# Selective scan on one core: Softplus summed in PSUM, a fifth of GpSimd's output multiplies on VectorE, a fourth scan buffer

## The chip, the cores and the metric

The kernel runs on one core of one Trainium2 chip. The metric is device time in microseconds (us) of one execution. A core has four engines that compute, each with a queue of its own that it works off in order: TensorE (PE in the profile; PEld is its weight load), VectorE (DVE), ScalarE (ACT) and GpSimd (POOL). A fifth, SyncE (SP), issues the DMAs here. [...]

## The reference

Sixteen images of 64 x 64 positions and 96 channels pass through two blocks.

The first block normalises, widens the image, squares it between two linear layers and narrows it again; the second block normalises, projects 96 channels to twice 192, convolves 3 x 3, applies SiLU, and then scans the image in four directions (rows, columns, and both reversed). In each direction there are 192 channels with 16 states each:

```
delta = softplus(dts + dt_bias)
h = exp(delta * A) * h + (delta * u) * B
y = sum over the 16 states of h * C
```

B, C and dts are linear in the image and differ from position to position. The four directions are added, normalised, gated with SiLU(z) and projected back to 96 channels.

## The kernel before, in words

`front(mi)` makes the first block, the convolution and z of image mi; `finish(mi)` makes the normalisation, gate and projection of its scan; `scan()` runs over all sixteen images and takes the largest part of the time. While it scans image mi, `front(mi + 1)` and then `finish(mi - 1)` run in the background.

**The scan's units.** An image is scanned in 8 steps (pair 0 forwards over four stretches of T = 1024 positions, pair 1 backwards). A step has 6 blocks (`blocks`, L601), a block has NQ = 4 groups (L705). So there are 16 x 8 x 6 x 4 = 3072 groups, numbered n. A group holds 128 partitions (32 channels times 4 states) by two halves e = 1 and e = 0 by 1024 positions. For each group:

- `drive(n)`, L731: GpSimd multiplies dtu by B into the buffer b, both halves at once (128x2048). The pool of b has three buffers (L613).
- `decay(n, e)`, L725: ScalarE makes da = exp(delta * a) for a half, into one of two PSUM tiles.
- `recur(n, e, out)`, L740 forwards and L742 backwards: VectorE's scan instruction over a half. For e = 1 the states go over b in SBUF, for e = 0 over da in PSUM.
- `keep(n, e, h)`, L748: ScalarE copies the last state of the half for the next stretch, one element per partition. The last of the four stretches needs none.
- The multiply by C: GpSimd for e = 1, in place in b (L877); VectorE for e = 0, from da into b (L887).
- `read_out(n)`, L764: TensorE adds the states up with a 0/1 matrix, 16 matmuls (y in PSUM over the four groups of a block; for pair 1 an identity matmul, L757, first puts in the partial sum y0 of pair 0). `store(n)`, L775, copies y out once per block.

**The order.** Instructions are put in each engine's queue as the Python code runs. The loop at L833 does, for group n: scan e=1, its keep, decay (n+1, 1), read-out of n-1, the multiply on GpSimd, drive n+2; then scan e=0, the multiply on VectorE, its keep, decay (n+1, 0). A drive has to wait for the read-out that frees its buffer.

**Positions.** At three places in each group `slot(0)`, `slot(1)` and `slot(2)` advance the background work by one `yield` each: first the step's own generator, `project` (L622), which makes rows (B and C), delta and dtu of the next step, then `front` or `finish`. `project` works in two halves of TB = 512 positions. In each half: load three tiles u (L634), three positions, matmul pp (L640), one position, pr (L643), and then for three tiles v: matmul s (L650), Softplus, dtu and delta to DRAM (L676, L677). So there are 128 x 2 x 3 = 768 such tiles.

**Softplus** is computed as max(s, 0) + log(1 + e) plus a correction e - ((1 + e) - 1) for the rounding of 1 + e, with e = exp(-|s|): ScalarE makes Abs, Exp, Ln and 1 + e (L658 to L661, L666); VectorE does the rest (L664, L668, L669) and multiplies by u (L672).

**Loads.** Everything goes through SyncE's queue in the order of the code. `fetch` brings dtu and delta of the next block, spread over the 128 partitions; `fetch_bc` brings a row block of B or C; `fetch_y0` brings the partial sum. In `front`, the narrowed rows s come from DRAM in two SBUF tiles of 44 and 20 rows (L408 to L416).

Of the kernel before, what the change touches and what calls it, by code (L numbers as in the profile page):

```python
# [74 lines left out]
PSLICES = 60  # L75


@with_exitstack
def tile_two_blocks(
# [103 lines left out]
    b12 = ctx.enter_context(tc.tile_pool(name="b12", bufs=1))  # L183
# [56 lines left out]
    def front(mi):  # L240
# [72 lines left out]
        for p0 in range(0, UPS, PP):  # L313
# [94 lines left out]
        JS = 44  # L408
        s = [
            b18.tile([UPS, JS, C], F32, name="s0", tag="b18"), b12.tile([UPS, HW - JS, C], F32, name="s1", tag="b12")  # L410
        ]
        for _ in range(2):
            yield
        for i, n, first in [(0, JS // 4, k * JS // 4) for k in range(4)] + [(1, 10, 0), (1, 10, 10)]:
            nc.sync.dma_start(out=s[i][:, first:first + n, :], in_=s_d[:, JS * i + first:JS * i + first + n, :])
            yield  # L416
# [4 lines left out]
        for j0 in range(0, HW + 8, 8):  # L421
            if done is not None:
                nc.scalar.activation(
                    x1v[:, :, j0 - 8:j0], done.rearrange("c w h -> c h w"), AF.Identity, bias=shift
                )
            if j0 < HW:
# [5 lines left out]
                for j in range(8):  # L432
                    nc.tensor.matmul(
                        done[:, j, :], lhsT=s[(j0 + j) // JS][:, (j0 + j) % JS, :], rhs=down_s, start=False, stop=True,
                        skip_group_check=True,
                    )
# [169 lines left out]
    def scan():  # L606


        with ExitStack() as es:
# [3 lines left out]
            p3 = es.enter_context(tc.tile_pool(name="sc_3", bufs=3))  # L613
# [8 lines left out]
            def project(mi, pair, lc, out):  # L622
# [6 lines left out]
                xs_d = image[mi]["xs"]  # L629
                for t in range(0, T, TB):  # L630
                    u = []
                    for v in range(3):
                        uv = up_.tile([128, TB], F32, name="u")
                        nc.sync.dma_start(out=uv, in_=xs_d[v, :, lc * T + t:lc * T + t + TB])  # L634
                        u.append(uv)
                    for _ in range(3):
                        yield
                    pp = gps.tile([128, TB], F32, name="pp", tag="g")
                    for v in range(3):
                        nc.tensor.matmul(pp, lhsT=xpt_s[:, pair, v, :], rhs=u[v], start=(v == 0), stop=(v == 2))  # L640
                    yield
# [4 lines left out]
                    for i, v in enumerate((0, 2, 1)):  # L646
# [10 lines left out]
                        e, d = (pj.tile([128, TB], F32, name=k) for k in ("e", "d"))  # L657
                        nc.scalar.activation(e, s, AF.Abs)  # L658
                        nc.scalar.activation(e, e, AF.Exp, scale=-1.0)
                        yield  # L660
                        nc.scalar.activation(d, e, AF.Ln, bias=one_s)  # L661
                        for _ in range(2):
                            yield
                        nc.vector.scalar_tensor_tensor(d, s, 0.0, d, ALU.max, ALU.add)  # L664
                        yield
                        nc.scalar.activation(s, e, AF.Identity, bias=one_s)  # L666
                        yield
                        nc.vector.scalar_tensor_tensor(s, s, -1.0, e, ALU.add, ALU.subtract)  # L668
                        nc.vector.tensor_sub(s, d, s)  # L669
# [3 lines left out]
                        yield  # L673
# [3 lines left out]
                        nc.sync.dma_start(out=out["delta"][v][:, t:t + TB], in_=delta)  # L677

            def fetch(what, ctx, bi):

                v, s0, r = blocks[bi]
                t = p2.tile([128, 2, T], F32, name=what)
                for e in (1, 0):
                    nc.sync.dma_start(
                        out=t[:, e, :],
                        in_=ctx[what][v][32 * (s0 + e):32 * (s0 + e) + 32, :].unsqueeze(1).to_broadcast([32, NQ, T]),
                    )
# [40 lines left out]
            def drive(n):  # L728
                b = p3.tile([128, 2, T], F32, name="b")
# [14 lines left out]
            def keep(n, e, h):  # L744
                st, bi, j = units[n]
                if st % NT < NT - 1:
                    end = h[:, T - 1:T] if steps[st][1] == 0 else h[:, 0:1]
                    nc.scalar.copy(states[bi][1][:, e, j:j + 1], end)  # L748
# [84 lines left out]
            for n, (st, bi, j) in enumerate(units):  # L833
# [28 lines left out]
                elif j == 1:  # L862
                    if ahead:
                        ops["delta", m + 1] = fetch("delta", *ahead)
                    if n + NQ <= last and steps[units[n + NQ - 1][0]][1] == 1:
                        st2, bi2, _ = units[n + NQ - 1]
# [151 lines left out]
```

## Time and profile before

| | us |
|---|---|
| median of three runs | 21924.01 (21922.5 to 21927.97) |
| the profiled execution, its own time | 21910.69 |
| its span, first to last instruction | 21908.9 |
| GpSimd busy | 20900.4 |
| VectorE busy | 19849.9 |
| TensorE busy | 15342.2 |
| ScalarE busy | 13130.2 |

A row of the groups reads: line, engine, operation, output <- inputs, their shapes, how often | busy time in us, mean duration in ns | idle time of the engine just before, and what ended it. A row of the waits reads: who waited for whom: us in total, how often, the longest. A row of the timeline reads: start in us, duration in us, what, and in brackets the idle time before it. A row of the busy times in a stretch reads: the stretch, its length, then busy us and number of instructions of PE, PEld, DVE, ACT and POOL, the granted TensorE clock, the DMA share and GB/s. TensorE's fp32 matmuls leave two records each. The end of a matmul's record is modelled, so a busy TensorE is not one at its peak.

### The profile page before, as it was taken

What the parts mean: (1) busy time and instruction counts of PE and PEld (TensorE: products, weight loads), DVE (VectorE), ACT (ScalarE), POOL (GpSimd) and SP (SyncE); (2) the same over time, 40 slices, a digit from 0 to 9 for tenths busy, and PEclk for the clock granted to TensorE, in tenths of its full rate; (3) what the DMA queues carried; (4) which work ended last, traced back from release to release, by engine and by line L of the source; (5) the groups of instructions that cost most, each with busy time, mean ns of one, the idle gap of its engine ahead of it and who ended that gap; (6) DMA issues with size and microseconds to landing.
All of it is one profiled execution on the core that took longest, in us unless ns stands there. A gap on an engine that the chain in (4) does not pass through costs nothing.

```text
span 21908.9 us, 260666 instructions
## 1 busy us (share of the span) xinstructions
PE 15342.2 (70%) x92844; PEld 6324.7 (29%) x92844; DVE 19849.9 (91%) x12829; ACT 13130.2 (60%) x20854; POOL 20900.4 (95%) x6152
## 2 busy tenths in 40 slices
PE   6766767766777677777767677767777677677745
PEld 4322323232232322324233232322323223242211
DVE  0999999999999999999999999999999999999996
ACT  4665656666565665656656566665656656566543
POOL 0999999999999999999999999999999999999997
PEclk7776777877778777777877778777787877778856
DMA  2555565656656566565655656556565655656654
GB/s 80 190 191 188 193 214 194 209 195 200 205 191 215 189 206 201 192 215 192 207 198 194 214 192 209 196 201 206 193 211 189 210 199 198 206 195 208 210 177 134
DMA packets 1851895, 4276.30 MB, mean 195 GB/s; under 512 B 449118, under 2 KB 548350, under 8 KB 1848542
## 3 DMA queue, kind: packets, MB, share of 16 engines
q1 hardware_dynamic: 1850590, 4259.62, 58.1%
q8 instruction: 731, 11.98, 0.2%
q14 instruction: 574, 4.70, 0.1%
HBM read 3380.58 MB, written 878.18 MB: 194 GB/s over the span
## 4 chain that ended last, share of the span: by engine, by line
DVE 36%; POOL 19%; issue 18%; PE 9%; ACT 9%; DMA 7%; SPq 1%; POOLq 0%; DVEq 0%; ACTq 0%
POOL b L731 10%; POOL b L877 10%; DVE da L742 7%; DVE da L740 7%; DVE b L740 6%; DVE b L742 6%; DVE b L887 4%; ACT da L725 4%; DMA u<-xs_d 2%; DVE s L669 2%; DVE dtu L672 2%; DVE s L668 2%; PE y L764 1%; DMA ct<-rows 1%; PE pp L640 1%
## 5 line engine op out<-in xcount | busy, mean ns | idle before, releaser
L731 POOL TENSOR_TENSOR b<-dtu,bt 128x2048 f32<-128x2048 f32 x3072 | 13984.9, 4552 | 584.6 <-DMA dtu<-dtu_d 522.9
L725 ACT ACTIVATE da<-delta,a_s 128x1024 f32<-128x1024 f32 x6144 | 6853.5, 1116 | 2826.6 <-DVE b L887 1185.9
L877 POOL TENSOR_TENSOR b<-b,ct 128x1024 f32<-128x1024 f32 x3072 | 7309.1, 2379 | 259.8 <-ACT new L748 249.5
L764 PE MATMUL y<-b,fold_s 128*32 128x256 f32 x49152 | 4638.9, 492 | 4107.3 <-DVE b L887 3102.6
L887 DVE TENSOR_TENSOR b<-da,ct 128x1024 f32<-128x1024 f32 x3072 | 3752.6, 1222 | 84.5
L764 PEld LDWEIGHTS y<-b,fold_s 128*32 128x32 f32 x49152 | 1353.3, 126 | 7627.7 <-DVE b L887 4083.3
L740 DVE TENSOR_TENSOR_SCAN da<-da,new,b 128x1024 f32<-128x1024 f32 x1152 | 2694.3, 2339 | 252.3 <-ACT da L725 252.3
L740 DVE TENSOR_TENSOR_SCAN b<-da,new,b 128x1024 f32<-128x1024 f32 x1152 | 2698.0, 2342 | 174.1 <-POOL b L731 166.9
L742 DVE TENSOR_TENSOR_SCAN da<-da,new,b 128x1024 f32<-128x1024 f32 x1152 | 2693.8, 2338 | 172.9 <-ACT da L725 172.7
L742 DVE TENSOR_TENSOR_SCAN b<-da,new,b 128x1024 f32<-128x1024 f32 x1152 | 2697.1, 2341 | 151.6 <-POOL b L731 109.5
L748 ACT COPY new<-da 128x1 f32<-128x1 f32 x2304 | 362.3, 157 | 3028.5 <-DVE b L887 3023.2
L473 PE MATMUL c_ps<-xgp,wtap_s 96*128 96x512 f32 (+1 forms) x4608 | 1817.8, 675 | 168.9 <-ACT row L491 164.1
L650 PE MATMUL s<-pr,dtw_s 128*128 128x512 f32 x1536 | 1120.4, 819 | 557.8 <-ACT delta L674 516.7
L377 PE MATMUL o_ps<-w2c_s,hsq 128*100 128x96 f32 x9600 | 1205.3, 293 | 191.9 <-ACT hsq L348 180.1
L365 PE MATMUL h_ps<-xu,w1t_s 96*128 96x500 f32 x1920 | 1147.6, 700 | 244.2 <-ACT hsq L348 108.6
L748 ACT COPY new<-b 128x1 f32<-128x1 f32 x2304 | 432.6, 188 | 1445.7 <-DVE b L742 740.4
L377 PEld LDWEIGHTS o_ps<-w2c_s,hsq 128*100 128x100 f32 x9600 | 1119.5, 203 | 407.4 <-ACT hsq L348 227.7
L640 PE MATMUL pp<-u,xpt_s 128*128 128x512 f32 x1536 | 903.7, 734 | 224.2 <-DMA u<-xs_d 216.0
L742 DVE TENSOR_TENSOR_SCAN b<-da,b 128x1024 f32<-128x1024 f32 x384 | 876.7, 2283 | 133.2 <-ACT da L725 74.8
L473 PEld LDWEIGHTS c_ps<-xgp,wtap_s 96*128 96x128 f32 (+1 forms) x4608 | 631.9, 182 | 1193.3 <-issue 938.6
L740 DVE TENSOR_TENSOR_SCAN da<-da,b 128x1024 f32<-128x1024 f32 x384 | 875.8, 2281 | 106.9 <-ACT da L725 106.9
L742 DVE TENSOR_TENSOR_SCAN da<-da,b 128x1024 f32<-128x1024 f32 x384 | 876.0, 2281 | 105.0 <-ACT da L725 105.0
(120 smaller groups left out, 18077.1 us busy)
## 6 DMA issues: line engine op xcount, KB each, us to landing
dtu<-dtu_d SPq DMA_DIRECT2D x1536, 512.0 KB
delta<-delta_d SPq DMA_DIRECT2D x1536, 512.0 KB
bt<-rows SPq DMA_DIRECT2D x1024, 512.0 KB
ct<-rows SPq DMA_DIRECT2D x1024, 512.0 KB
u<-xs_d SPq DMA_DIRECT2D x896, 256.0 KB
dtu_d<-dtu SPq DMA_DIRECT2D x768, 256.0 KB
delta_d<-delta SPq DMA_DIRECT2D x768, 256.0 KB
xr<-in_x SPq DMA_DIRECT2D x768, 128.0 KB
```

What stands on the lines that cost most here:

```text
L365: nc.tensor.matmul(h_ps[j], lhsT=w1t_s[:, 128 * j:128 * (j + 1)], rhs=xu.rearrange("c p q -> c (p q)"), start=True, stop=True,)
L377: nc.tensor.matmul(o_ps[:, p, :], lhsT=hsq[j][:, UPS * p:UPS * (p + 1)], rhs=w2c_s[:, j, :], start=(j == 0), stop=(j == HB - 1),)
L473: nc.tensor.matmul(c_ps[p:p + n], lhsT=wtap_s[:, tap, 128 * i:128 * i + n], rhs=xgp[:, h0:h0 + 8, dx:dx + HW], start=(tap == 0), stop=(tap ...
L640: nc.tensor.matmul(pp, lhsT=xpt_s[:, pair, v, :], rhs=u[v], start=(v == 0), stop=(v == 2))
L650: nc.tensor.matmul(s, lhsT=dtw_s[:, pair, v, :], rhs=pr, start=True, stop=True)
L725: nc.scalar.activation(da, ops["delta", n // NQ][:, e, :], AF.Exp, scale=a_s[:, k, g, units[n][2]:units[n][2] + 1])
L731: nc.gpsimd.tensor_mul(b, ops["dtu", n // NQ], bt.unsqueeze(1).to_broadcast([128, 2, T]))
L740: nc.vector.tensor_tensor_scan(out, da, b, before, ALU.mult, ALU.add)
L742: nc.vector.tensor_tensor_scan(out[:, ::-1], da[:, ::-1], b[:, ::-1], before, ALU.mult, ALU.add)
L764: nc.tensor.matmul(y[32 * q:32 * q + 32, e, :], lhsT=fold_s, rhs=b[:, e, QT * q:QT * q + QT], start=(pair == 0 and j == 0 and e == 0), sto ...
L877: nc.gpsimd.tensor_mul(h, h, bc[1, r, j])
L887: nc.vector.tensor_mul(bs[n][:, 0, :], h, bc[1, r, j])
```

## The change

1. **Softplus.** VectorE's three instructions go. ScalarE makes m = max(s, 0) (Relu), w = 1 + e and then w = 1 - w; TensorE adds w + e + d + m in PSUM with four identity matmuls. VectorE multiplies the sum by u as before, and ScalarE copies it to delta in the same position.
2. **A shared multiply.** With `SHARE = 5`, in each group with n % 5 == 4 the e=1 scan writes into da (PSUM), and VectorE multiplies by C into b, in place of GpSimd.
3. **End states.** In the other groups VectorE copies the e=1 end state, in place of ScalarE.
4. **Read-out.** `read_out(n - 2)` takes the place of `read_out(n - 1)`, `store` follows it, and b has four buffers. y0 is asked for at the end of a block's last group, not in the second group of the block.
5. **Inputs.** `project` asks for u of the first half at once, for u of the second half as each tile v of the first half is done; three positions lie before pp, two after it.
6. **Space.** s passes through one SBUF tile in 40 and then 24 rows, fetched eight rows at a time, with five more positions between.

```diff
-        JS = 44
-        s = [
-            b18.tile([UPS, JS, C], F32, name="s0", tag="b18"), b12.tile([UPS, HW - JS, C], F32, name="s1", tag="b12")
-        ]
+        def fetch_s(first, n):
+            t = b18.tile([UPS, n, C], F32, name="s", tag="b18")
+            for k in range(0, n, 8):
+                nc.sync.dma_start(out=t[:, k:k + 8, :], in_=s_d[:, first + k:first + k + 8, :])
+                yield t, first
...
+            if j0 == JS:
+                for s, s_first in fetch_s(JS, HW - JS):
+                    yield
+                for _ in range(2):
+                    yield
...
-            p3 = es.enter_context(tc.tile_pool(name="sc_3", bufs=3))
+            p4 = es.enter_context(tc.tile_pool(name="sc_4", bufs=4))
...
+                order = (0, 2, 1)
+
+                def fetch_u(v, t):
+                    uv = up_.tile([128, TB], F32, name="u")
+                    nc.sync.dma_start(out=uv, in_=xs_d[v, :, lc * T + t:lc * T + t + TB])
+                    return uv
+
+                ahead_u = [fetch_u(v, 0) for v in order]
                 for t in range(0, T, TB):
-                    u = []
-                    for v in range(3):
-                        uv = up_.tile([128, TB], F32, name="u")
-                        nc.sync.dma_start(out=uv, in_=xs_d[v, :, lc * T + t:lc * T + t + TB])
-                        u.append(uv)
                     for _ in range(3):
                         yield
+                    u, ahead_u = dict(zip(order, ahead_u)), []
...
-                    yield
+                    for _ in range(2):
+                        yield
                     pr = pj.tile([128, TB], F32, name="pr")
...
                         nc.scalar.activation(e, s, AF.Abs)
                         nc.scalar.activation(e, e, AF.Exp, scale=-1.0)
                         yield
+                        nc.scalar.activation(m, s, AF.Relu)
+                        nc.scalar.activation(w, e, AF.Identity, bias=one_s)
+                        yield
                         nc.scalar.activation(d, e, AF.Ln, bias=one_s)
-                        for _ in range(2):
-                            yield
-                        nc.vector.scalar_tensor_tensor(d, s, 0.0, d, ALU.max, ALU.add)
-                        yield
-                        nc.scalar.activation(s, e, AF.Identity, bias=one_s)
-                        yield
-                        nc.vector.scalar_tensor_tensor(s, s, -1.0, e, ALU.add, ALU.subtract)
-                        nc.vector.tensor_sub(s, d, s)
+                        nc.scalar.activation(w, w, AF.Identity, scale=-1.0, bias=one_s)
+                        yield
+                        s = gps.tile([128, TB], F32, name="s", tag="g")
+                        yield
+                        for k, of in enumerate((w, e, d, m)):
+                            nc.tensor.matmul(s, lhsT=ident_s, rhs=of, start=(k == 0), stop=(k == 3))
+                        for _ in range(2):
+                            yield
                         dtu = pj.tile([128, TB], F32, name="dtu")
                         delta = pj.tile([128, TB], F32, name="delta")
                         nc.vector.tensor_mul(dtu, s, u[v])
-                        yield
                         nc.scalar.copy(delta, s)
                         yield
                         nc.sync.dma_start(out=out["dtu"][v][:, t:t + TB], in_=dtu)
                         nc.sync.dma_start(out=out["delta"][v][:, t:t + TB], in_=delta)
+                        if t + TB < T:
+                            ahead_u.append(fetch_u(v, t + TB))
...
-                h = bs[n][:, 1, :]
+                odd_here = n % SHARE == SHARE - 1
+                h = das[n, 1] if odd_here else bs[n][:, 1, :]
                 recur(n, 1, h)
-                keep(n, 1, h)
+                if odd_here:
+                    nc.vector.tensor_mul(bs[n][:, 1, :], h, bc[1, r, j])
+                keep(n, 1, h, nc.scalar.copy if odd_here else nc.vector.tensor_copy)
                 if n < last:
                     decay(n + 1, 1)
-                if n:
-                    read_out(n - 1)
+                if n >= 2:
+                    read_out(n - 2)
                 slot(0)
-                nc.gpsimd.tensor_mul(h, h, bc[1, r, j])
+                if not odd_here:
+                    nc.gpsimd.tensor_mul(h, h, bc[1, r, j])
...
-                if n and units[n - 1][2] == NQ - 1:
-                    storing = store(n - 1)
+                if n >= 2 and units[n - 2][2] == NQ - 1:
+                    storing = store(n - 2)
                     next(storing)
...
-                keep(n, 0, h)
+                keep(n, 0, h, nc.scalar.copy)
...
+                if j == NQ - 1 and n < last and steps[units[n + 1][0]][1] == 1:
+                    st2, bi2, _ = units[n + 1]
+                    y0s[steps[st2][2], bi2] = fetch_y0(steps[st2][2], bi2)
```

## The prediction

> **What bounds the kernel now.** I read the page's busy times first, then the groups by line, then what VectorE and GpSimd waited for, then the timeline of a stretch with no background work, and last the busy times in two stretches with much of it.
>
> ```profile
> PE 15342.2 (70%) x92844; PEld 6324.7 (29%) x92844; DVE 19849.9 (91%) x12829; ACT 13130.2 (60%) x20854; POOL 20900.4 (95%) x6152
> ```
>
> GpSimd is at 95% of the whole span, and the first 513 us and the last 164 us have no scan in them (the first drive starts at 513.3 us, the last GpSimd multiply ends at 21745.4 us). Of the 21232 us between, it works 20900.4 - 35 = 20865 us, 98%. VectorE works 19849.9 - 51 = 19799 us there, 93%.
>
> ```profile
> L731 POOL TENSOR_TENSOR b<-dtu,bt 128x2048 f32<-128x2048 f32 x3072 | 13984.9, 4552 | 584.6 <-DMA dtu<-dtu_d 522.9
> ...
> L877 POOL TENSOR_TENSOR b<-b,ct 128x1024 f32<-128x1024 f32 x3072 | 7309.1, 2379 | 259.8 <-ACT new L748 249.5
> ...
> L650 PE MATMUL s<-pr,dtw_s 128*128 128x512 f32 x1536 | 1120.4, 819 | 557.8 <-ACT delta L674 516.7
> ...
> L669 DVE TENSOR_TENSOR s<-d,s 128x512 f32<-128x512 f32 x768 | 534.5, 696 | 26.2
> ...
> L668 DVE SCALAR_TENSOR_TENSOR s<-s,e 128x512 f32<-128x512 f32 x768 | 521.3, 679 | 22.6 <-ACT s L666 22.6
> L664 DVE SCALAR_TENSOR_TENSOR d<-s,d 128x512 f32<-128x512 f32 x768 | 517.7, 674 | 277.3 <-ACT d L661 250.6 <-ACT new L748 24.6
> ```
>
> GpSimd has two instructions per group. Their records overlap a little; the timeline shows the true steps:
>
> ```profile
> 21579.73 4.77 POOL L731 TENSOR_TENSOR b<-dtu,bt 128x2048 f32<-128x2048 f32 x1
> ...
> 21584.20 2.60 POOL L877 TENSOR_TENSOR b<-b,ct 128x1024 f32<-128x1024 f32 x1
> ...
> 21584.53 2.35 DVE L742 TENSOR_TENSOR_SCAN b<-da,new,b 128x1024 f32<-128x1024 f32 x1 [0.92 <-POOL b L731]
> ...
> 21586.51 4.78 POOL L731 TENSOR_TENSOR b<-dtu,bt 128x2048 f32<-128x2048 f32 x1
> ...
> 21586.80 2.33 DVE L742 TENSOR_TENSOR_SCAN da<-da,new,b 128x1024 f32<-128x1024 f32 x1
> ...
> 21589.17 1.23 DVE L887 TENSOR_TENSOR b<-da,ct 128x1024 f32<-128x1024 f32 x1
> ...
> 21590.98 2.62 POOL L877 TENSOR_TENSOR b<-b,ct 128x1024 f32<-128x1024 f32 x1
> ```
>
> A multiply by C takes 86.51 - 84.20 = 2.31 us, a drive 4.47 us, a group 6.78 us with no gap on GpSimd; VectorE needs 2.27 + 2.37 + 1.2 = 5.86 us and waits 0.92 us for the drive. The average over the scan is 21232 / 3072 = 6.91 us, so all stalls together cost 0.13 us a group.
>
> ```profile
> DVE da L740 <- ACT da L725: 359.2, 285, 5.9
> ...
> DVE da L742 <- ACT da L725: 277.6, 267, 2.4
> ...
> POOL b L877 <- ACT new L748: 249.5, 168, 4.0
> ...
> POOL b L731 <- PE y L764: 15.9, 17, 2.5
> ```
>
> VectorE's waits for a late decay (359.2 + 277.6 for e=0, 114.8 + 27.1 for e=1: 779 us) are covered today by its own slack. GpSimd hardly ever waits for a buffer: 15.9 us.
>
> ```profile
> 9149.00:9314.00 165.00, 129.61 (x573) 48.06 (x571) 144.14 (x93) 114.62 (x169) 154.56 (x46) 0.90 0.54 188
> ...
> 9483.00:9754.00 271.00, 229.54 (x957) 67.81 (x957) 263.40 (x180) 148.75 (x227) 268.18 (x80) 0.85 0.68 222
> ```
>
> The columns are PE, PEld, DVE, ACT and POOL. The first row lies in the convolution, the second in the previous image's ending. TensorE is busy 79% and 85%, and in the convolution GpSimd has already fallen to 94%: by the drives' starts 24 groups took 7.2 us each.
>
> [...]
>
> ```profile
> L236 DVE TENSOR_TENSOR nb<-nmean,rg x32: 155/499/1320, 38.8 to 19752.2; 96x1 f32<-96x1 f32 x32
> L258 DVE TENSOR_TENSOR shift<-k_ps,cb_s x16: 124/125/155, 39.5 to 19169.9; 96x1 f32<-96x1 f32 x16
> ```
>
> Both handle one element per partition. With both inputs in SBUF (L236) it takes 155 ns while GpSimd is idle, 0.49 or 1.3 us beside a multiply; by the start times it then ends where GpSimd's instruction ends. With one input in PSUM it takes 125 ns. [...] no table load for the new activations. That is not shown here, but the existing Abs and Identity beside Exp and Ln load none.
>
> **The change part by part.**
>
> GpSimd. Every fifth group's e=1 multiply leaves: 614 x 2.31 = -1418 us. Floor: 20865 - 1418 = 19447 us, 6.33 us a group.
>
> VectorE. Away: L664, L668 and L669, 1573.5 us by the rows, about 1450 us after the overlap of neighbouring records. Added: 614 multiplies at 1.2 us = 740 us. Added: the e=1 end states of ordinary groups, 3/4 x 4/5 of 3072 = 1843 one-element copies. Each waits for its own engine's scan, as the e=0 multiply does (step 2.37 instead of 2.27 us: 0.1), and costs 0.05 (L258's step to its successor) to 0.125 us itself: 0.15 to 0.22, I take 0.19, 350 us. The odd groups' multiply waits for its scan too: 614 x 0.1 = 60. Floor: 19799 - 1450 + 740 + 350 + 60 = 19500 us. So both engines end level, each at 6.34 us a group, and a stall of either that was covered before is covered no longer.
>
> The two can drift apart without loss: scan (n, 1) may start after drive n, and GpSimd needs it 2.31 + 4.47 us later, so with 2.35 us of scan there are 4.4 us of play. A shifted group costs VectorE 7.1 against GpSimd's 4.47, a swing of 2.6, or 3.3 with a 0.69 us dtu in it. It fits.
>
> ScalarE. Added per tile: Relu (0.58 us, like Abs, L658) and twice an Identity (0.67, like L666); away L666: +1.25 x 768 = 960 us; away 1843 end states at 0.19: -350. 13130 becomes 13740, of 20500: 67%. Below nothing this can't be; its price is lateness. Three positions now hold two activations each (1.2 to 1.4 us), and queued behind them is the next decay, for which the e=0 scan waits. Between the end of a scan (n, 1) and the time decay (n+1, 0) can start lie 3.5 us, in which 1.12 us of decay and two positions must fit. I add 200 us to the 779 (0 to 500).
>
> The inputs' part works against that. By the start times, 265 of the 637 us of e=0 waits lie in groups 2 and 12 of the step, where the projection waits for u (216.0 us of PE waits on that load). Second-half inputs are now asked for as their buffers come free, three positions or more ahead, and pr comes one position later. I take the 265 away. Stalls from ScalarE: 779 - 265 + 200 = 715 us.
>
> TensorE. Four identity matmuls per tile; 128x512 fp32 has two records, 0.43 us from start to start when dense, 0.53 often: 768 x 4 x 2 x 0.43 to 0.53 = 2640 to 3260 us, about 1.1 us a group. In the second stretch above TensorE needs 229.5 / 40 = 5.74 us a group; less 0.16 for the tail of an isolated matmul's record and plus 1.1 it needs 6.7, more than 6.33. About two fifths of an image's groups look like that (conv and ending, part of the upsampling): 0.4 x 3072 x 0.4 = 490 us, at least 0 since a TensorE that idles less also waits less. Part falls together with the stalls above: I take 300.
>
> The later read-out with a fourth buffer removes PE waits on b (3102.6 + 989.8 us), and 15.9 us of GpSimd's; drive n+2 still waits for the same place in TensorE's queue. Nothing by itself. Removing the end state from ScalarE takes GpSimd's 249.5 us away; it is inside the 6.91, not in my floor.
>
> SyncE. The same loads of u, issued between stores; y0 two groups later, with two still to go before its use (13 us), its wait for the old y0's matmul (128.7 us) gone; s in 40 + 24 rows through one buffer, two more DMAs and five more positions per image. The second fetch waits on its queue for the first 40 rows' matmuls, a few us, with the state and operand loads behind it; those are issued two groups ahead. The background of an image ends at group 183 of 192 now, so there is room. All at nothing; if the cover is gone, some 5 us x 15.
>
> Sum: 19500 + 715 + 300 = 20515 us of scan, 6.68 a group; + 513 + 164 + 2 outside the span = 21194, against this execution's own 21910.7; the median of the runs shown is 13 us above that. Forecast: 21200 us, 3.3% less.
>
> **The rivals.**
> 1. Everything is hidden: TensorE's additional work fits where it waits for VectorE today, and the decays come in time. For it: 6200 us of PE idle in the scan. Against it: the two level floors. 19500 + 400 + 692 = 20600 us (20500 to 20850).
> 2. TensorE becomes the bound in the dense stretches and pulls ScalarE along: 490 us and 300 more by late results, 500 instead of 200 for bunching: 21200 + 190 + 300 = 21700 us (21450 to 21880). For it: 0.94 in the convolution already.
> 3. Slower: [...] Then it waits for the end of GpSimd's instruction, as L236 does. VectorE's slack in ordinary groups is lost: GpSimd's multiply follows the copy (0.15 us of gap in three of five groups), and at a shifted group VectorE needs 13.1 us from there to the next copy, GpSimd only 2.5 + 4.47 + 4.47 = 11.4. Five groups: 4 x 6.78 + 4.47 + 0.45 + 1.9 = 33.9 us, 6.78 each, 20830 us; with the 715 and half the TensorE term 21700 + 692 = 22390 us (21950 to 22600). It decides as soon as the mean wait per copy exceeds some 0.5 us. [...]
>
> **How the numbers follow.** Forecast 0.53 (20850 to 21450), rival 1 0.14, rival 2 0.17, rival 3 0.13, others on the slow side 0.03. The range from 20600 to 21900 leaves out the lower half of rival 1 and rival 3, under 2 in 10. A difference under 0.2%, 44 us, can't be told from none: faster 0.83, same 0.03, slower 0.14.
>
> **What would show it.** Right: GpSimd's multiplies 2458, its share 93% to 96% with waits on scans rather than on end states; VectorE 94% or more; the copies under 0.13 us; VectorE's waits for decays 600 to 900 us; group pace 6.5 in quiet stretches and about 7 in the convolution. Wrong: copies with a mean of 0.5 us and more (rival 3); GpSimd waiting for PE's read-out, or ScalarE for PE in the hundreds of us (rival 2); a scan below 20000 us (rival 1).

## The result: 0.8% slower, with both floors where they were forecast

The changed kernel takes 22098.04 us (22080.05 to 22100.75), the kernel before 21925.0 us in the same runs: a ratio of 1.0077, 95% interval 1.0061 to 1.0093. The forecast was 21200 us. The scan now lasts from the first drive at 540.8 us to 21927.9 us, 21387 us or 6.96 us a group (before 21232 and 6.91).

The page's busy times of the changed kernel:

```profile
PE 17043.2 (77%) x98988; PEld 7377.7 (33%) x98988; DVE 19484.8 (88%) x12983; ACT 13747.4 (62%) x20546; POOL 19521.3 (88%) x5538
```

GpSimd lost 1379 us of work (1418 were forecast), and the time did not follow: it fell from 95% busy to 88%. No engine is at its limit. So the change exchanged work on the busiest engine for idle time on two engines at once. In the scan GpSimd idles 1866 us between its multiplies (332 before) and VectorE 1931 us (1423 before). The groups of the page, of the changed kernel:

```profile
L750 POOL TENSOR_TENSOR b<-dtu,bt 128x2048 f32<-128x2048 f32 x3072 | 13900.4, 4531 | 1692.0 <-PE y L783 969.3
...
L897 POOL TENSOR_TENSOR b<-b,ct 128x1024 f32<-128x1024 f32 x2458 | 5797.0, 2358 | 714.1 <-DVE new L767 478.8
...
L682 PE MATMUL s<-w,ident_s 128*128 128x512 f32 x1536 | 1202.4, 875 | 1388.1 <-ACT w L677 1275.5
...
L687 DVE TENSOR_TENSOR dtu<-s,u 128x512 f32<-128x512 f32 x768 | 527.0, 686 | 668.2 <-PE s L682 666.1
```

The last figure of each row is the idle time that one releaser ended. The drive, which hardly waited for a buffer before (15.9 us), now waits 969 us for TensorE's read-out. VectorE's dtu waits 666 us for the new sum on TensorE: 199 us of it for the six tiles of the first projection, before the scan starts, and 467 us inside the scan. VectorE's waits for the decays, of the changed kernel:

```profile
DVE da L759 <- ACT da L744: 661.2, 468, 13.4
DVE da L761 <- ACT da L744: 338.7, 285, 3.3
...
DVE b L761 <- ACT da L744: 192.9, 118, 2.9
```

They have grown as well. With a last row of 30.9 us they add up to 1224 us. Split by half with the order of the scans in the trace, the e=0 half waits 943 us (637 before) and the e=1 half 281 us (142 before). Busy times of the changed kernel in three stretches of one image (length, then busy us and instructions of PE, PEld, DVE, ACT, POOL, then the granted TensorE clock, DMA share and GB/s). The first two hold the same groups, to within one at an edge, as the prediction's two stretches, the third is the image's end, with little background:

```profile
9257.00:9423.00 166.00, 142.16 (x590) 58.20 (x592) 136.33 (x94) 118.79 (x161) 138.83 (x40) 0.90 0.50 171
9585.00:9857.00 272.00, 241.58 (x1037) 79.65 (x1037) 263.35 (x180) 161.18 (x232) 254.78 (x73) 0.95 0.67 222
9857.00:9934.00 77.00, 46.79 (x258) 15.50 (x254) 76.32 (x48) 42.70 (x59) 76.37 (x23) 0.76 0.64 210
```

At the end of the image VectorE and GpSimd are both at 99%: there the exchange works (over all images the last twelve groups take 6.42 us each, before 6.79). In the convolution, the first row, TensorE is at 86%, VectorE at 82% and GpSimd at 84%: everybody waits for somebody.

**Two places where the time is lost.** The timeline of the changed kernel in one group (start, duration, what; in brackets the idle time before it and its releaser):

```profile
10006.48 2.28 DVE L759 TENSOR_TENSOR_SCAN b<-da,b 128x1024 f32<-128x1024 f32 x1
...
10008.79 1.12 ACT L744 ACTIVATE da<-delta,a_s 128x1024 f32<-128x1024 f32 x1 [2.04 <-DVE b L759]
...
10009.94 2.30 DVE L759 TENSOR_TENSOR_SCAN da<-da,b 128x1024 f32<-128x1024 f32 x1 [1.00 <-ACT da L744]
...
10015.00 0.34 PEld L682 LDWEIGHTS s<-w,ident_s 128*128 128x128 f32 x1 [0.50 <-issue]
...
10020.41 1.02 PE L682 MATMUL s<-m,ident_s 128*128 128x512 f32 x2
...
10021.47 0.69 DVE L687 TENSOR_TENSOR dtu<-s,u 128x512 f32<-128x512 f32 x1 [2.29 <-PE s L682]
...
10022.20 1.07 PE L783 MATMUL y<-b,fold_s 128*32 128x256 f32 x16
...
10023.39 4.53 POOL L750 TENSOR_TENSOR b<-dtu,bt 128x2048 f32<-128x2048 f32 x1 [3.30 <-PE y L783]
```

In the first three rows ScalarE stands idle for 2.04 us, not busy with something else, and starts the decay of half 0 when the scan of half 1 ends; then VectorE waits almost the whole length of that Exp. Both decays of the group stand in the same one of the two PSUM places (a place is the stretch of PSUM that a tile is given). Which place a tile gets is decided by the build: in the built program the two halves share one in 606 of 3072 groups (529 before, mostly groups 2, 3, 8, 12, 15 and 18 of a step). The traces agree: in the changed kernel all 606 of these groups have an e=0 wait, 656 of the 943 us; of the other 2466 groups 112 have one, 287 us. In the kernel before, groups that share a place have 547 of the 637 us.

The other rows are the new sum. TensorE loads its first weight at 10015.00 and ends at 10021.43; dtu waits 2.29 us in VectorE's queue with the C-multiply and the next scan behind it, and the read-outs wait in TensorE's queue with the drive's buffer behind them.

### The profile page after: what moved, and what is told of

Its sections match the earlier page's. It is cut to its first block, busy times and chain, and to the rows that moved or that the text cites. A ratio compares the mean times of both kernels' runs of the same rounds, so it can differ in the third digit from the quotient of the medians.

```text
span 22094.2 us, 273189 instructions
## 1 busy us (share of the span) xinstructions
PE 17043.2 (77%) x98988; PEld 7377.7 (33%) x98988; DVE 19484.8 (88%) x12983; ACT 13747.4 (62%) x20546; POOL 19521.3 (88%) x5538
## 5 line engine op out<-in xcount | busy, mean ns | idle before, releaser
L897 POOL TENSOR_TENSOR b<-b,ct 128x1024 f32<-128x1024 f32 x2458 | 5797.0, 2358 | 714.1 <-DVE new L767 478.8
L783 PE MATMUL y<-b,fold_s 128*32 128x256 f32 x49152 | 3689.9, 426 | 555.7 <-DVE b L907 367.1
L759 DVE TENSOR_TENSOR_SCAN da<-da,new,b 128x1024 f32<-128x1024 f32 x1383 | 3248.2, 2349 | 557.4 <-ACT da L744 555.9
L761 DVE TENSOR_TENSOR_SCAN da<-da,new,b 128x1024 f32<-128x1024 f32 x1382 | 3243.3, 2347 | 166.7 <-ACT da L744 160.0
L682 PE MATMUL s<-w,ident_s 128*128 128x512 f32 x1536 | 1202.4, 875 | 1388.1 <-ACT w L677 1275.5
L761 DVE TENSOR_TENSOR_SCAN b<-da,new,b 128x1024 f32<-128x1024 f32 x922 | 2158.0, 2341 | 43.7 <-ACT da L744 42.7
L759 DVE TENSOR_TENSOR_SCAN b<-da,new,b 128x1024 f32<-128x1024 f32 x921 | 2156.3, 2341 | 8.2 <-ACT da L744 8.2
L761 DVE TENSOR_TENSOR_SCAN da<-da,b 128x1024 f32<-128x1024 f32 x461 | 1056.3, 2291 | 179.9 <-ACT da L744 178.7
L377 PE MATMUL o_ps<-w2c_s,hsq 128*100 128x96 f32 x9600 | 1050.1, 269 | 154.0 <-ACT hsq L348 144.8
L759 DVE TENSOR_TENSOR_SCAN da<-da,b 128x1024 f32<-128x1024 f32 x460 | 1053.6, 2290 | 107.5 <-ACT da L744 105.3
L662 PE MATMUL s<-pr,dtw_s 128*128 128x512 f32 x1536 | 891.2, 663 | 327.8 <-ACT delta L688 172.0
L687 DVE TENSOR_TENSOR dtu<-s,u 128x512 f32<-128x512 f32 x768 | 527.0, 686 | 668.2 <-PE s L682 666.1
L682 PE MATMUL s<-e,ident_s 128*128 128x512 f32 x1536 | 1072.7, 790 | 0.0
```

Source lines behind the costliest of these rows:

```text
L377: nc.tensor.matmul(o_ps[:, p, :], lhsT=hsq[j][:, UPS * p:UPS * (p + 1)], rhs=w2c_s[:, j, :], start=(j == 0), stop=(j == HB - 1),)
L682: nc.tensor.matmul(s, lhsT=ident_s, rhs=of, start=(k == 0), stop=(k == 3))
L759: nc.vector.tensor_tensor_scan(out, da, b, before, ALU.mult, ALU.add)
L761: nc.vector.tensor_tensor_scan(out[:, ::-1], da[:, ::-1], b[:, ::-1], before, ALU.mult, ALU.add)
L783: nc.tensor.matmul(y[32 * q:32 * q + 32, e, :], lhsT=fold_s, rhs=b[:, e, QT * q:QT * q + QT], start=(pair == 0 and j == 0 and e == 0), sto ...
L897: nc.gpsimd.tensor_mul(h, h, bc[1, r, j])
```

## The experiments

Two theories to begin with. **Places**: decays that share a PSUM place with their group's other half. **Sum**: four matmuls in one piece, with other work behind them in two queues. The kernel before, measured anew in five sets of runs, took 21914 to 21927 us, so a difference of some 10 us between two rows means nothing.

| kernel | us | ratio to before, 95% |
|---|---|---|
| changed kernel | 22098 | 1.0077 (1.0061 to 1.0093) |
| changed + separate places | 21615 | 0.9858 (0.9843 to 0.9873) |
| changed, two of four matmuls | 21259 | 0.9696 (0.9681 to 0.9710) |
| changed, Softplus as before | 22487 | 1.0258 (1.0241 to 1.0275) |
| before + separate places | 21836 | 0.9960 (0.9945 to 0.9974) |
| changed + places, two of four matmuls | 20946 | 0.9555 (0.9540 to 0.9569) |
| changed + places + split sum | 21147 | 0.9649 (0.9633 to 0.9665) |
| changed, inputs together as before | 22099 | 1.0080 (1.0065 to 1.0095) |
| changed, read-out of n - 1 | 22089 | 1.0076 (1.0061 to 1.0091) |
| changed, end states on ScalarE | 21976 | 1.0028 (1.0016 to 1.0040) |
| places + split, six positions to pp | 21293 | 0.9715 (0.9700 to 0.9729) |
| places + split, one odd group in eight | 21374 | 0.9750 (0.9736 to 0.9765) |
| before + new Softplus | 22381 | 1.0214 (1.0198 to 1.0229) |
| before + new Softplus + places | 22055 | 1.0057 (1.0042 to 1.0072) |
| places + split, end states on ScalarE | 21056 | 0.9600 (0.9586 to 0.9615) |
| places + split, fourth input buffer | 21019 | 0.9588 (0.9574 to 0.9603) |
| the last two together | 20916 | 0.9541 (0.9525 to 0.9557) |

### Separate places

```diff
-            aps = es.enter_context(tc.tile_pool(name="sc_aps", bufs=2, space=PSUM))
+            aps = es.enter_context(tc.tile_pool(name="sc_aps", bufs=1, space=PSUM))
...
-                da = aps.tile([128, T], F32, name="da")
+                da = aps.tile([128, T], F32, name="da", tag=f"da{e}")
```

It takes the same PSUM space, one place for each half. In the changed kernel:

> The changed kernel, with one PSUM slot for the decay of each half (tag da0, da1; one buffer each) in place of two slots for both. Theory slots: in the built program of the changed kernel the e=0 decay of 606 groups stands in the slot of the same group's e=1 decay, so it can't begin before that scan ends and the e=0 scan waits for a whole Exp; with fixed slots VectorE's waits for decays before e=0 scans fall from about 950 us to under 250 and the time to 21000 to 21400 us. Theory matmul sum (the four identity matmuls of Softplus delay VectorE's queue and the read-outs): the waits move to dtu and to the read-outs, and the time stays at 21800 us or more.

In the kernel before:

> The kernel before with one PSUM slot for the decay of each half. Theory slots: there 529 groups share a slot too, VectorE's e=0 waits of 637 us fall to under 150, but GpSimd is the bound, so the time falls by 100 to 250 us only. Theory matmul sum: it moves by less than 60 us.

The waits of the changed kernel with separate places:

```profile
DVE dtu L687 <- PE s L682: 709.5, 306, 134.2
DVE da L759 <- ACT da L744: 329.0, 170, 14.0
...
DVE da L761 <- ACT da L744: 183.1, 138, 3.3
```

The e=0 waits halve, from 943 to 463 us, and the time falls by 483 us, while the wait for the sum stays. That is less than the places theory expected (waits under 250 us, 21400 us or less) and more than the sum theory allowed, so the places are one loss but not the only one. In the kernel before, the e=0 waits fall from 637 to 232 us, but the time by 90 us only, again short of the 100 to 250 of the places theory: there VectorE had slack (its waits for the drive grow instead, from 383 to 650 us), and GpSimd's idle time fell by only 78 us. One shared place cost 90 / 529 = 0.17 us before and 483 / 606 = 0.80 us after.

### The sum

Two of the four matmuls alone, (d, m), where d is log(1 + e), with w and its two activations left out; this leaves out the correction for the rounding of 1 + e:

> The changed kernel with two identity matmuls per tile (d and m) in place of four; it leaves out the correction w + e for the rounding of 1 + e, and with it two ScalarE activations per tile. Theory matmul sum: GpSimd's waits for read-outs fall from 969 to under 500 us, VectorE's waits before dtu from 666 to under 250 us, the time is 21300 to 21600 us. Theory slots: the e=0 waits stay at 800 us or more and the time stays at 21800 us or more.

The Softplus of the kernel before, in the changed kernel:

> The changed kernel with the Softplus of the kernel before (three VectorE instructions per tile, no identity matmuls), all else as changed. VectorE's floor rises to 19456 + 1450 = 20900 us. Theory matmul sum: the stalls of the matmuls go, VectorE is the bound with few stalls, the time is 21600 to 21900 us, less than the changed kernel's. Theory slots: the e=0 waits of some 900 us come on top of the higher floor, the time is 22300 us or more.

Leaving two out brings 839 us, a little more than the sum theory expected; the drive's wait for the read-out falls to 360 us and dtu's wait to 224. But the e=0 waits fall too, to 622 us: in the built program of this kernel only 394 groups share a place, so the edit changed the places as well. Going back to VectorE's three instructions costs 389: VectorE is then busy for 20859 us of the scan, 1403 more, and idle for 938. So the 21600 to 21900 us that the sum theory expected of it were wrong: the sum's stalls are real, but smaller in this kernel than the work that it takes off VectorE. The time fits the places theory, but its reason does not: the e=0 waits are 425 us instead of some 900, and only 261 groups share a place here.

Both cures at once, and then a cure that leaves no work out:

> The changed kernel with a PSUM place of its own for each half's decay and with only two of the four identity matmuls (the correction of the logarithm and its two activations are left out). If the shared places and the long sum on TensorE are two separate losses, their gains add: 22098 - 483 - 839 = 20776, 20700 to 20870, with the decay waits of the second half near 450 us and dtu's wait for the sum near 220 us. If they are two names of one stall (a late group that either cure brings back), no more than a third of the smaller gain is left: 21080 to 21260.

```diff
                         s = gps.tile([128, TB], F32, name="s", tag="g")
+                        for k, of in enumerate((e, m)):
+                            nc.tensor.matmul(s, lhsT=ident_s, rhs=of, start=(k == 0), stop=False)
                         yield
-                        for k, of in enumerate((w, e, d, m)):
-                            nc.tensor.matmul(s, lhsT=ident_s, rhs=of, start=(k == 0), stop=(k == 3))
+                        for k, of in enumerate((w, d)):
+                            nc.tensor.matmul(s, lhsT=ident_s, rhs=of, start=False, stop=(k == 1))
```

> The changed kernel with a PSUM place of its own for each half's decay and with all four identity matmuls, but the two of exp(-|s|) and max(s,0), which are ready early, issued one position ahead of the other two. TensorE's work is the same. If what costs is that one long piece of TensorE work stands between the last activation and dtu, with the read-outs behind it, then halving the piece brings about half of what leaving two matmuls out brought (839 us, of which the two activations and the issue of matmuls are a part): 21150 to 21450 against 21615 of the kernel with the places alone, and dtu's wait for the sum falls from 710 us to below 500. If it is TensorE's total work, or ScalarE's two extra activations, that costs: 21560 to 21650, and TensorE's wait for the activation w stays near 1150 us.

The two cures bring 1152 us together against 483 + 839 = 1322 apart: mostly two losses, with 170 us in common, so that the time lies above the one expectation and below the other. The places can account for the common part: with two matmuls left out 606 - 394 = 212 fewer groups share one, which at 0.80 us each is an estimated 170 us. With the places separate, leaving out two matmuls and their activations is worth 21615 - 20946 = 669 us. The split brings 468 of these 669 us (21615 to 21147), with no work left out, 3 us past the lower end of its expectation. Waits with separate places and the split sum:

```profile
DVE dtu L689 <- PE s L684: 309.9, 94, 131.1
...
DVE da L761 <- ACT da L746: 285.1, 152, 11.7
DVE da L763 <- ACT da L746: 172.6, 130, 3.6
```

Inside the scan, without the six tiles before it, dtu's wait falls from 511 us to 127. TensorE has the same 98988 matmuls, and now nothing but (w, d) stands between the last activation and dtu. From the first record's start to the last one's end the whole piece took 4.73 us on average in the changed kernel; the second piece takes 2.01 us here. So most of what the sum costs is the length of the piece that others wait for, not TensorE's load. How the other 201 us divide between two matmuls and two activations was not tried.

### The new Softplus on the kernel before

> The kernel before with the new Softplus alone (activations, four identity matmuls on TensorE, nothing else of the change). VectorE loses 1450 us of work, but GpSimd keeps its 20865 us. The first theory, that a late sum costs only where both engines are at their limit: 21800 to 22000, GpSimd's idle time within 100 us of the 332 us of the kernel before. The rival, that the sum on TensorE costs by itself whatever the other engines do, since the read-outs behind it hold the drive's buffer: 22200 to 22700, with GpSimd's wait for the read-out above 600 us.

It costs 466 us (22381 against 21914 of the kernel before in the same runs), although VectorE is relieved. The time lies in the rival's range and GpSimd's idle time rises to 768 us, so the first theory is out; but the rival's mechanism is not there either. The drive waits only 119 us for the read-out. The waits of this kernel:

```profile
DVE dtu L675 <- PE s L670: 899.5, 399, 134.5
DVE da L742 <- ACT da L727: 711.2, 530, 5.9
DVE da L744 <- ACT da L727: 532.9, 443, 2.5
```

The decays' waits are the largest of any kernel here, and in its built program the halves share a place in 870 groups. So the places are separated there too:

> The kernel before with the new Softplus alone and a PSUM place of its own for each half's decay. The Softplus alone cost 466 us, but it also moved the planner's places: the two halves of a group stand in one place in 870 groups there, in 529 before. If the 466 us are the sum's own (dtu waits for TensorE in VectorE's queue): 22150 to 22350, since the places alone brought the kernel before only 90 us. If they are mostly the places: 21800 to 22000.

The result, 22055, lies between the two expectations. The places were worth 326 us of it. Against the kernel before with separate places (21836) 219 us stay with the sum: GpSimd idles 432 us instead of 254 (+179), and the scan starts 27 us later, since the first projection, which nothing overlaps, now takes longer.

### Read-out and inputs

```diff
-                if n >= 2:
-                    read_out(n - 2)
+                if n:
+                    read_out(n - 1)
```

(with the store moved back likewise, and the four buffers kept)

> The changed kernel with the read-out of the previous group in each group, as before, but with the four buffers kept. The prediction held that the later read-out is worth nothing because the driving multiply still waits for the same place in TensorE's queue. If so that wait (969 us in the changed kernel) is what the later read-out costs here: with the earlier read-out and four buffers the driving multiply has a group more of slack, its wait for the read-out falls below 400 us and the time to 21700 to 22000. If instead the later read-out frees TensorE from waiting for the C-multiplies, the earlier one brings those waits back in front of the sum and the projection: 22150 to 22400, with dtu's wait for the sum above 700 us.

22089 us: no difference from 22098, and neither expectation met. GpSimd's waits with the earlier read-out, the three longest but for the first load:

```profile
POOL b L897 <- DVE new L767: 1106.8, 560, 7.0
...
POOL b L897 <- DVE b L759: 274.8, 95, 10.5
POOL b L897 <- issue: 193.6, 97, 4.8
```

The drive's 969 us for the read-out are gone (5.4 left), and the C-multiply waits for VectorE's scan instead; GpSimd's idle time is 1868 us, before 1866. In the same run TensorE's wait for u falls from 660 to 167 us. By these names 1513 of the 1868 us end with an instruction of VectorE, so the read-out was merely the door at which GpSimd stood waiting for VectorE.

Inputs loaded together at the head of each half, as before:

> The changed kernel with the three inputs of a chunk loaded together at the head of the chunk, as before the change. If the early, one by one loads are what makes TensorE's projection wait (660 us, before 216) and this holds the read-outs and so GpSimd: 21750 to 22000, with the projection's wait near 220 us. If the wait grew because the stores ahead of the loads in SyncE's queue wait for a later dtu, the order of the loads is indifferent: 22050 to 22150, and the wait stays above 500 us.

22099 us, and TensorE's wait for u stays at 697 us: the order of the loads is indifferent. More lead was then tried in two ways. First, six positions instead of three before pp, the early matmuls moved up one position in exchange:

> The changed kernel with separate PSUM places and the split sum, and with six positions instead of three between the inputs and the projection; the three are taken from the Softplus of the three directions (the two early identity matmuls go one position earlier), so that a chunk has as many positions as before. TensorE's wait for the inputs (689 us) is in most chunks a few us, but once in each image it is over 12 us and the decays stand behind it by way of ScalarE. If those long waits are on the path: 20900 to 21080, and the wait for the inputs falls below 200 us. If they are covered, or the inputs are late by SyncE's queue and not by the number of positions: 21110 to 21180.

It is 146 us slower than the split kernel, outside both ranges. The waits of TensorE and VectorE with six positions:

```profile
PE s L680 <- ACT m L673: 1023.5, 520, 6.0
...
DVE dtu L688 <- PE s L683: 455.2, 231, 131.3
...
PE pp L651 <- DMA u<-xs_d: 68.4, 18, 12.6
```

The inputs are in time, but (e, m) now stands in TensorE's queue before m is ready (608 us before this edit), and dtu waits 145 us more: the position taken away was worth more than the lead. The second way leaves the positions alone:

```diff
-            up_ = es.enter_context(tc.tile_pool(name="sc_u", bufs=3))
+            up_ = es.enter_context(tc.tile_pool(name="sc_u", bufs=4))
...
+                    if t + TB < T:
+                        ahead_u.append(fetch_u(order[0], t + TB))
...
-                        delta = pj.tile([128, TB], F32, name="delta")
+                        delta = d
...
-                        if t + TB < T:
-                            ahead_u.append(fetch_u(v, t + TB))
+                        if t + TB < T and i < 2:
+                            ahead_u.append(fetch_u(order[i + 1], t + TB))
```

> The kernel with separate places and the split sum, and a fourth input buffer (it takes the place of one Softplus tile, delta standing where the logarithm was), so that each input of the second chunk is loaded one direction earlier and the positions of everything else stay. With six positions of lead the inputs no longer kept TensorE waiting but the sum came out later. If the long waits for inputs are on the path: 20920 to 21080, and TensorE's wait for them falls below 350 us. If they are covered: 21110 to 21190.

It brings 128 us, and TensorE's wait for u falls from 689 to 253 us; the e=0 waits of group 12 of a step fall from 152 us to none. So late inputs do cost, some of them: in the split kernel at 1077 us pp waits 12.4 us for u, the matmuls e_ps of the background stand behind it, ScalarE's activation xt behind those, and a decay behind that; VectorE then waits 8.8 us.

### End states and the share

All end states on ScalarE again (`nc.scalar.copy` in both calls of `keep`):

> The changed kernel with all end state copies on ScalarE. The prediction put the 1843 copies on VectorE at 350 us. If they are no more than that and VectorE's floor counts: 21750 to 21950, VectorE's busy time lower by about 285 us and GpSimd's wait for the first half's scan no longer, 300 us or less. If the copies go unnoticed because the C-multiply of GpSimd starts on time all the same: 22060 to 22130. If they relieve ScalarE, whose decays come late without them: 22150 to 22350, with the decay waits above 1300 us.

> The kernel with separate places and the split sum, and all end state copies on ScalarE. The copies take VectorE some 285 us; putting them back brought 122 us in the changed kernel. If VectorE's floor now decides, with its stalls halved: 20900 to 21040. If ScalarE is short of time here (the decays come later): 21100 to 21250.

It brings 122 us in the changed kernel and 91 us with places and split; both times lie a little above the range of the floor theory. VectorE's busy time falls by 291 us, and part comes back as later decays (e=0 waits 943 to 1075 us in the changed kernel). The C-multiply still waits, 967 us now, under the name of the ScalarE copy, where the floor theory put 300 us or less: again the door, not the cause.

`SHARE = 8` with places and split:

> The changed kernel with separate PSUM places and the split sum, and one odd group in eight on VectorE instead of one in five: 230 multiplies of 2.35 us go back to GpSimd, which then has 541 us more work, and VectorE some 240 us less. If the two engines' stalls are one another's, since neither has slack where both are 92% busy, then with slack on VectorE GpSimd's idle time falls from 947 us to 350 to 600 and the time is 21250 to 21400. If GpSimd's idle time is its own, it stays and the work is added: 21620 to 21720.

227 us slower, within the first expectation's range. GpSimd gets 514 us more work and idles 320 us less (947 to 627, where 350 to 600 were expected). So some 60% of the added work went into time in which GpSimd had stood idle, as it would if VectorE's stalls had held it up there; the rest is added. Of the two shares one in five is the better.

Both remaining gains together:

> Both of the last two edits on the kernel with separate places and the split sum. If they act on different waits, their gains add: 20720 to 20950. If each only moves the other's wait: within 60 us of the better of the two.

They add: 21147 - 91 - 128 = 20928, measured 20916.18 us (20898.28 to 20936.62), 4.6% below the kernel before, with the whole computation. Its busy times:

```profile
PE 16771.1 (80%) x98988; PEld 7175.0 (34%) x98988; DVE 19165.4 (92%) x11139; ACT 13943.8 (67%) x22390; POOL 19511.8 (93%) x5538
```

## Why the prediction was wrong, step by step

**GpSimd's floor, 19447 us: right, to 74 us.** 2458 multiplies, and 19521 us busy in the scan. The prediction took 35 us of GpSimd's work for work outside the scan; by the trace it was 0.5 us.

**VectorE's floor, 19500 us: right.** Its busy time is 19456 us; the prediction's steps also held the short gaps between a scan and its follower, 63 us before the copies and 45 us before the odd multiplies: 19564. The copies were put at 350 us and took 284 + 63 = 347; the odd multiplies at 800 and took 797. The source line of the copies in the changed kernel (shortest, median and longest in ns):

```profile
L767 DVE COPY new<-b x1844: 153/154/157, 547.8 to 21775.0; 128x1 f32<-128x1 f32 x185
```

No copy took longer than 157 ns, and 1361 of them lie wholly inside a GpSimd multiply, so rival 3 is out: none was held up beside GpSimd for 0.49 or 1.3 us, as L236 was in the kernel before. L236 reads two inputs from SBUF, the copy reads one. The kernel before has no copy of one element on VectorE, so the price of 0.05 to 0.125 us for the copy itself was an estimate from L258. What the step missed is that such a floor isn't paid in full: 347 us on VectorE, 122 or 91 us of time.

**ScalarE's stalls, 715 us: wrong, and the main error beside the next.** ScalarE's work came out as worked out (13740 forecast, 13747 measured), and the new activations loaded no table: both traces have 389 table loads, none of them on a line of Softplus. The decay waits are 943 + 281 = 1224 us. The step that failed is "265 of the 637 us of e=0 waits lie in groups 2 and 12 of the step, where the projection waits for u ... I take the 265 away". TensorE's wait for u in the changed kernel, which was 216.0 us before:

```profile
PE pp L651 <- DMA u<-xs_d: 660.0, 213, 24.0
```

The new order of the loads did not bring u in time, and groups 2 and 12 still have 216 of the 943 us. And u was only part of the cause. Separating the PSUM places alone takes 405 of the 637 us away in the kernel before, 150 of the 265 among them; what late inputs do cost, the fourth input buffer shows. The prediction did not look at the places at all. The row of the decay waits says who came last, and ScalarE was read as late; the timeline shows it idle, waiting for the other half's scan.

**TensorE's term, 300 us: wrong in mechanism and size.** It priced the sum as load ("dense stretches") and let it vanish elsewhere. Inside the scan dtu alone waits 467 us. With the places separate, halving the piece brings 468 us with the same load, and leaving half of it out, with two activations, 669 us. Asking what is queued behind the new wait, as the prediction did for ScalarE, would have found it: dtu stands in VectorE's queue ahead of the C-multiply and the next scan, the read-outs in TensorE's. The load, too, was low: 768 x 4.73 = 3630 us of pieces against 2640 to 3260.

**The coupling.** "A stall of either that was covered before is covered no longer" was written down, but then only the old stalls were added up. The same place-sharing costs 0.17 us before and 0.80 us after; between these two kernels that factor is what a lost slack is worth. Slack on VectorE alone does not decide it: in the kernel before with the new Softplus, where VectorE idles most, it was 326 / 870 = 0.37 us.

**Read-out: "nothing by itself", right** (22089 against 22098). **SyncE "at nothing": right** as far as the time goes: with the inputs loaded as before it is the same, 22099 us. For s TensorE's matmuls waited 19 us in 11 waits, "a few us" each as forecast. **The start:** the scan begins at 540.8 instead of 513.3 us; the sum of the prediction kept 513.

The account: floor +64, start +28, stalls (1931 - 108 = 1823 against 1015) +808; together 900 of the 902 us between the prediction's sum, 21194, and the profiled execution, 22096.

**The prediction's own signs.** The count of the multiplies came out. The copies took 0.154 us where it wrote under 0.13, GpSimd and VectorE are at 88% where it wrote 93% and 94% or more, and the decay waits lie above its 600 to 900.

**The rivals.** Rival 1 fails with the idle times. Rival 2's marks are there (GpSimd waits for the read-out; ScalarE waits for TensorE: 298 us for e_ps, 273 for xu_ps, 247 for s), but its own mechanism isn't: TensorE is no bound where the same load in two pieces runs at 6.66 us a group instead of 6.80. Rival 3 gave the right sign, and even a range that holds the result, for a wrong reason: luck. What stays open: how the remaining 701 us of GpSimd's idle time in the best kernel divide.

## What to carry to other kernels

When a change brings a second engine up to the first one's load, price every stall of both anew, also those that cost little before: here one shared place cost 0.17 us before and 0.80 us after, and both engines idled longer, GpSimd 1866 us (332 before) and VectorE 1931 us (1423). Where a wait names an engine, look in the timeline whether that engine was busy or itself idle, and whom it waited for; buffers that a planner places for you can be the answer (separate places brought 483 us here), and an edit elsewhere can move them (606 groups shared a place, and 394 with two matmuls left out). So look at the places before you credit an edit with its gain. And when a reduction moves to another engine, look at the piece that is left after its last input: here two of the four terms, issued one position earlier, brought 468 us with the same load. Issue the early terms first.

## What was not expected of the hardware

**TensorE started slowly after a pause.** In the sum of the changed kernel a third of the steps from one matmul record to the next took over 0.7 us (typically 0.85), the others 0.43. Of the 150 sums before which TensorE's matmuls had paused for over 4 us, 147 began with a slow step; of the 392 after less than 1 us, 132. The trace's record of the granted clock goes with it: 1799 of the 1800 slow steps lie where it says 0.5, 3463 of the 3576 others where it says 1.0. With the sum split, 26% of the steps of the first piece are slow, but only 4% of the second, which follows a few us later. So the short bursts between waits were dearer here than the dense price of the same matmuls: 0.59 us a step on average in the sum of the changed kernel, against 0.43 us.

**One wait under several names.** Undoing the read-out's delay moved 969 us from one name to others in GpSimd's waits, with its idle time the same to 2 us.
